# A symmetric block matrix built in pairs: the second sum of a pair goes into the tile of a loaded block

## The chip, the cores and the metric

The kernel runs on one NeuronCore of a Trainium2 chip. The metric is the device time of one execution in microseconds (us). The median of four runs before the change is 1603.98 us (1599.13 to 1610.67). The engines are named as in the profile: PE is TensorE (matmuls; PEld its weight loads), DVE is VectorE, ACT is ScalarE, POOL is GpSimd, SP is SyncE, which here only issues DMAs.

## What is computed

A graph convolution with a residual and a layer norm. Cut to what matters:

```python
HW = einsum('bnf,fo->bno', x, W)            # x: 8 x 4096 x 256, W: 256 x 256
A_norm = relu((A + A.T) * 0.5)              # A: 4096 x 4096, mostly zeros
D = sum(A_norm, axis=1)
d = where(D > 0, D ** -0.5, 0)
L_norm = eye(N) - d[:, None] * A_norm * d[None, :]
out = relu(einsum('nm,bmo->bno', L_norm, HW))
result = layernorm(x + out)
```

All numbers are float32 (f32).

## The kernel before

It has two large stages.

**Stage one** reads A in blocks of 512 by 512 (an 8 by 8 grid; one block is 1 MB and one tile of 128 partitions by 4 times 512 numbers) and writes relu((A + A.T)/2) into a scratch matrix in device memory, `a_dram`. The loop runs over the block row i and, inside it, over j from i to 7. For j > i the two blocks (i,j) and (j,i) are handled together and are called a pair here. One pair goes like this:

- `load_adj` loads the blocks, `tij` first and `tji` second, from SP's DMA queue (line 350), into the pool `adj` of four buffers. For j = i there is one load, and `tji` is `tij`.
- `symmetrise` forms one sum: for each of the four row strips of a block, PE transposes four 128 by 128 pieces of the opposite block into one bank of PSUM (line 360), and DVE adds the block's own strip to it (line 364), into the sum's tile. The transposes take banks from four of the tag `b0`, which other matmuls share, so PE can be at most four strips ahead of DVE.
- `keep` then takes the finished sum: ACT applies the relu with factor 0.5 in place (line 368), DVE reduces it to the sums of groups of 64 columns, `part` (line 369), ACT's DMA queue stores it to `a_dram` (line 375), and for j = i POOL copies the diagonal pieces to `diag`.

Each sum has a tile of its own in the pool `sym` of three buffers, so a pair takes two. The sum of block (i,j) comes first and that of (j,i) second; both are formed before `keep` is called for either, but with other work recorded between (below). A buffer is free again for a load or a sum when everything that reads or writes its old tile is done; a store counts until it has landed.

Beside each pair stand matmuls that don't depend on it. `form` makes 128 rows of x times W: two loads of x (line 451, SP's queue for i below 4, POOL's from i = 4 on), transposes on PE (`xtr`, line 458), copies by ACT (`xt`, line 459), matmuls (`pg`, line 469), and the eviction by ACT. Where the degree of these rows is known the eviction scales by r (`gt`, line 479) and the result is stored to `g_dram`; the last ten strips (22 to 31) are formed early, kept unscaled (`held`, line 481) and scaled once r is known (`release`, lines 492 and 494). `multiply` adds up the product for the first 128 rows of the output (`lead`, line 427), one strip at a time. For i below 4 there is about one `form` per pair, from i = 4 on two.

After row i, `degrees(i)` sums row i of `part` (line 386) and makes r with a power on POOL (line 389), and `lower_diagonal` subtracts from the diagonal pieces and stores them. In rows 3 and 4 `spread_early` makes index lists for stage two in tiles that it takes from the same two pools: `hot` from `sym`, `mixed` from `adj`.

The order on each engine is not written by hand in stage one: a scheduler sets it from the recorded order and its own estimate of times. On an engine and on its DMA queue, instructions are issued strictly in that order, so a load that waits for its buffer holds up what stands behind it. The DMAs of SP and ACT take one of eight completion semaphores in turn, and each waits until the DMA that had the semaphore before it has landed.

**Stage two** starts when `a_dram` and `g_dram` are complete. For each 128 rows of the output it gathers the nonzero rows by indirect DMAs from POOL (lines 733 and 744) and multiplies (`py`, line 933), and applies the residual and the layer norm.

Of the kernel before, what the change touches and what calls it, by code (L numbers as in the profile page):

```python
# [9 lines left out]
F32 = mybir.dt.float32  # L10
# [34 lines left out]
def kernel(  # L45
# [28 lines left out]
    P = 128  # L74
    S = 512
    A = S // P
# [100 lines left out]
    def patterns(u):  # L177

        used = ipool.tile([P, QU, NB], F32, tag="used", name=f"used_{u}", bufs=1)
        nb = blocks(u)  # L180
        if nb == 1:
            nc.vector.memset(used, 0.0)
        lo = (2 * u + 1) * 2
        nc.vector.tensor_scalar(
            used[:, : 2 * nb],
            part[:, :, lo : lo + 2 * nb].rearrange("p m s -> p s m"),
            0.0,
            None,
            ALU.is_gt,
        )  # L190
        diag = used[:, :, 2 * u + 1 : 2 * u + 1 + nb]
        nc.vector.tensor_tensor(diag, diag, own[:, :, :nb], ALU.max)
        two = ipool.tile([P, 2, NB], F32, tag="two", name=f"two_{u}", bufs=1)
        uv = used.rearrange("p (b h) m -> p b h m", b=2)
        nc.vector.scalar_tensor_tensor(two, uv[:, :, 1], 2.0, uv[:, :, 0], ALU.mult, ALU.add)
        pat = ipool.tile([P, NB], F32, tag="pat", name=f"pat_{u}")
        nc.vector.scalar_tensor_tensor(pat, two[:, 1], 4.0, two[:, 0], ALU.mult, ALU.add)
        kind = ipool.tile([P, NK, NB], BF16, tag="kind", name=f"kind_{u}")
        nc.vector.tensor_tensor(
            kind,  # L200
            pat.unsqueeze(1).to_broadcast([P, NK, NB]),
            kinds.unsqueeze(2).to_broadcast([P, NK, NB]),
            ALU.is_equal,
        )
        plan[u] = pat, kind
# [128 lines left out]
    with (  # L334
# [13 lines left out]
        def load_adj(i, j):  # L348
            t = apool.tile([P, A, S], F32, tag="adj", name=f"adj_{i}_{j}")
            nc.sync.dma_start(  # L350
                t,
                adj[i * S : (i + 1) * S, j * S : (j + 1) * S].rearrange("(a p) s -> p a s", p=P),
            )
            return t

        def symmetrise(i, j, tij, tji, sym):
            for a in range(A):
                pt = psum.tile([P, S], F32, tag="b0", name=f"tr_{i}_{j}_{a}")
                for c in range(A):
                    ins = nc.tensor.transpose(  # L360
                        pt[:, c * P : (c + 1) * P], tji[:, c, a * P : (a + 1) * P], ident
                    )
                done_pe.append(ins.ins)
                nc.vector.tensor_add(sym[:, a, :], pt, tij[:, a, :])  # L364
                yield

        def keep(i, j, sym, diag):
            nc.scalar.activation(sym, sym, AF.Relu, scale=0.5)  # L368
            nc.vector.tensor_reduce(  # L369
                part[:, i * A : (i + 1) * A, j * S // Q : (j + 1) * S // Q],  # L370
                sym.rearrange("p a (c q) -> p a c q", q=Q),
                AX.X,
                ALU.add,
            )
            nc.scalar.dma_start(
                a_dram[i * S : (i + 1) * S, j * S : (j + 1) * S].rearrange("(a p) s -> p a s", p=P), sym
            )
            if i == j:
                for a in range(A):
                    nc.gpsimd.tensor_copy(diag[:, a, :], sym[:, a, a * P : (a + 1) * P])  # L380

        def degrees(i):
            ms = slice(i * A, (i + 1) * A)
            deg = stat1.tile([P, A], F32, tag="deg", name=f"deg_{i}")
            none = stat1.tile([P, A], F32, tag="none", name=f"none_{i}")
            nc.vector.tensor_reduce(deg, part[:, ms, :], AX.X, ALU.add)
            nc.vector.tensor_scalar(none, deg, 0.0, None, ALU.is_le)
            nc.vector.tensor_add(e[:, ms], deg, none)  # L388
            nc.gpsimd.tensor_tensor(r[:, ms], e[:, ms], neg_half[:, :A], ALU.pow)  # L389
            nc.vector.tensor_scalar(minus_r[:, ms], r[:, ms], -1.0, None, ALU.mult)  # L390
# [34 lines left out]
        def multiply(m, g, strip):  # L425
            for c in range(G // S):
                nc.tensor.matmul(  # L427
                    lead[c],
                    lhsT=strip,
                    rhs=g[:, c * S : (c + 1) * S],  # L430
                    start=not done,
                    stop=len(done) == NB - 1,
                    skip_group_check=True,
                )
                yield
            done.append(m)
# [63 lines left out]
        def release_all(i):  # L500
            for m in range(i * A, (i + 1) * A):
                if m in held:
                    release(m)
            lower_diagonal(i, diags.pop(i))
# [8 lines left out]
        def run_due(flush=False):  # L513
            for d in due:
                d[0] -= 1
            while due and (flush or due[0][0] <= 0):
                _, fn, args = due.pop(0)
                fn(*args)
# [29 lines left out]
        for i in range(NS):  # L548
            diag = stat1.tile([P, A, P], F32, tag="diag", name=f"diag_{i}")
            for j in range(i, NS):  # L550
                tij = load_adj(i, j)
                tji = load_adj(j, i) if j > i else tij
                parts = [(i, j, tij, tji)] + ([(j, i, tji, tij)] if j > i else [])
                parts = [(p, spool.tile([P, A, S], F32, tag="sym", name=f"sym_{p[0]}_{p[1]}")) for p in parts]
                credit += (1.0 if j > i else 0.5) * (1 if i < 4 else 2)
                beside = [multiply(*args) for args in waiting]
                waiting.clear()
                products = len(beside)

                some = i < NS - 2 or i == j  # L560
                while some and credit >= 1.0 and (known or early):
                    beside.append(form(known.pop(0), True, i >= 4) if known else form(early.pop(0), False))
                    credit -= 1.0
                    some = i < NS - 2
                credit = min(credit, 1.0)
                for p, sym in parts:
                    for _ in symmetrise(*p, sym):
                        pass
                if i == NS - 1:


                    release_all(i - 1)
                    beside = beside[products:] + beside[:products]
                for n, b in enumerate(beside):
                    with tc.issue_after(done_pe[-1]) if i == NS - 1 and n < 2 else nullcontext():
                        for _ in b:
                            pass
                for (rows, cols, _, _), sym in parts:
                    keep(rows, cols, sym, diag)
                run_due()  # L580
            degrees(i)
            diags[i] = diag
            if i != NS - 2:
                release_all(i)
            known += range(i * A, min((i + 1) * A, NB - HOLD))
            if i == 1:
                for n, u in enumerate(SEQ[:2]):
                    patterns(u)
                    due += [[2 + n, count_place, (u,)], [4 + n, count_place_rest, (u,)]]
                due.sort(key=lambda d: d[0])  # L590
            elif i == 2:
                for n, u in enumerate(SEQ[2:4]):
                    patterns(u)
                    due.append([1 + n, count_place, (u,)])
                due.append([3, count_place_rest, (SEQ[2],)])
            elif i < 5 and i > 2:

                pieces = spread_early(SEQ[i - 3])
                for n in range(5):
                    due.append([1 + n // 2, next, (pieces, None)])  # L600
                due.append([4, collect_index, (SEQ[i - 3],)])
# [10 lines left out]
    def residual(i, ypool):  # L612
        xr = ypool.tile([P, B, F], F32, tag="xr", name=f"xr_{i}", bufs=4)
        ins = nc.scalar.dma_start(xr, x[:, i * P : (i + 1) * P, :].rearrange("b p f -> p b f"))
        return xr, ins.ins
# [343 lines left out]
    with tc.If(short > 0):  # L959
        with (  # L960
# [4 lines left out]
            for i in range(NB):  # L965
# [17 lines left out]
                z, _ = residual(i, ypool)  # L983
# [30 lines left out]
```

## Time and profile before

The profiled execution took 1604.0 us; its span, from the first to the last instruction of the core, is 1602.3 us.

| engine | busy us | share of the span | instructions |
|---|---|---|---|
| PE matmul | 1498.1 | 93% | 6544 |
| PE weight loads | 779.8 | 49% | 6544 |
| DVE | 890.9 | 56% | 2250 |
| ACT | 371.6 | 23% | 462 |
| POOL | 759.8 | 47% | 1109 |

| stage | window, us | PE busy us | DVE busy us | DMA share | GB/s |
|---|---|---|---|---|---|
| one | 0 to 575 | 527.65 | 362.47 | 0.97 | 359 |
| two | 575 to 1603 | 970.49 | 528.46 | 0.95 | 359 |

The mean granted clock of TensorE is 0.972. The DMA share is the mean busy share of the core's 16 DMA engines, from the time that their packets took; it can come out a little above 1.

What the steps of stage one cost each:

| line | step | count | mean ns |
|---|---|---|---|
| L360 | PE transpose, 128x128 | 1024 | 285 |
| L364 | DVE addition, 128x512 | 256 | 683 |
| L368 | ACT relu, 128x2048 | 64 | 1914 |
| L369 | DVE reduction, 128x2048 to 128x32 | 64 | 2278 |
| L469 | PE matmul, 128x256 | 1024 | 383 |
| L427 | PE matmul `lead`, 128x512 | 176 | 593 |

Each of the 64 loads of A and each of the 64 stores to `a_dram` moves 1024 KB.

### The profile page before, as it was taken

To read this page: it belongs to the slowest core of one execution; us is meant where nothing else is said; L and a number is where in the kernel's file an instruction comes from. 1 tells how busy PE (TensorE), PEld (TensorE's weight loads), DVE (VectorE), ACT (ScalarE), POOL (GpSimd) and SP (SyncE) were. 2 spreads that over 40 slices of the span, in tenths; PEclk is the share of its full clock that TensorE was granted. 3 is DMA by queue.
4 is the path that set the end of the run, shared out by engine and by line. 5 is a ranking of instruction groups with operands and counts; after the bars stand their busy time and mean duration, and the time that the engine had idled before them with its cause. 6 is when DMAs were issued, how large, how long until landed. Compare 5 with 4: busy or idle time off the path is not lost.

```text
span 1602.3 us, 18959 instructions
## 1 busy us (share of the span) xinstructions
PE 1498.1 (93%) x6544; PEld 779.8 (49%) x6544; DVE 890.9 (56%) x2250; ACT 371.6 (23%) x462; POOL 759.8 (47%) x1109
## 2 busy tenths in 40 slices
PE   6999989998899898999999998899999998999984
PEld 5778877777677633333333333234333342333331
DVE  5665668876474604355384493571085655657542
ACT  3555554554344500101001000010001101010111
POOL 3001010102123256576776676676576666666662
PEclk9999999999999998999999999899999998999997
DMA  9999999999889899999999999999899999999994
GB/s 355 367 362 404 389 363 377 398 391 367 291 325 330 343 356 403 355 389 347 404 368 367 377 372 357 374 386 362 322 347 346 345 377 361 377 384 374 361 342 157
DMA packets 222037, 575.71 MB, mean 359 GB/s; under 512 B 20403, under 2 KB 108771, under 8 KB 184195
## 3 DMA queue, kind: packets, MB, share of 16 engines
q0 software_dynamic: 59552, 316.19, 51.3%
q10 hardware_dynamic: 72032, 134.51, 22.2%
q1 hardware_dynamic: 90352, 123.74, 22.0%
q8 instruction: 54, 0.88, 0.2%
q14 instruction: 47, 0.39, 0.1%
HBM read 479.07 MB, written 136.34 MB: 384 GB/s over the span
## 4 chain that ended last, share of the span: by engine, by line
PE 74%; DMA 12%; DVE 8%; issue 3%; ACT 2%; POOL 0%; SPq 0%; ACTq 0%; DVEq 0%; POOLq 0%
PE py L933 53%; PE pg L469 10%; DMA a_dram<-sym 5%; PE lead L427 5%; DMA g<-g_dram,gi 3%; DVE sym L364 3%; PE xtr L458 3%; PE tr L360 3%; DMA adj<-in_adj_dram 2%; DVE part L369 1%; DMA xin<-in_x_dram 1%; ACT sym L368 1%; DMA xr<-in_x_dram 1%; PE lists L295 1%; ACT xt L459 0%
## 5 line engine op out<-in xcount | busy, mean ns | idle before, releaser
L933 PE MATMUL py<-g,ga 128*64 128x512 f32 (+1 forms) x3152 | 946.1, 603 | 38.9 <-issue 24.4
L933 PEld LDWEIGHTS py<-g,ga 128*64 128x64 f32 (+1 forms) x3152 | 343.2, 154 | 630.2 <-issue 602.1
L744 POOL DMA_INDIRECT g<-g_dram,gi x302 | 339.1, 1123 | 238.3 <-issue 76.4
L733 POOL DMA_INDIRECT ga<-a_dram,ai x302 | 331.5, 1098 | 99.7 <-issue 86.5
L631 DVE TENSOR_TENSOR xr<-xr,y 128x2048 f32<-128x2048 f32 x31 | 71.1, 2294 | 452.9 <-ACT y L620 378.7
L620 ACT ACTIVATE y<-py,minus_r 128x512 f32<-128x512 f32 x120 | 80.5, 687 | 889.2 <-PE py L933 837.4
L469 PE MATMUL pg<-w_sb,xt 128*128 128x256 f32 x1024 | 230.8, 383 | 5.3 <-ACT xt L459 5.2
L364 DVE TENSOR_TENSOR sym<-tr,adj 128x512 f32<-128x512 f32 x256 | 163.3, 683 | 112.5 <-PE tr L360 93.0
L469 PEld LDWEIGHTS pg<-w_sb,xt 128*128 128x128 f32 x1024 | 194.4, 193 | 33.7 <-ACT xt L459 6.0
L369 DVE TENSOR_REDUCE part<-sym 128x32 f32<-128x2048 f32 x64 | 145.4, 2278 | 62.4 <-ACT sym L368 62.4
L360 PE MATMUL tr<-ident,adj 128*128 128x128 f32 x1024 | 137.6, 285 | 24.4 <-DVE sym L364 12.0
L389 POOL TENSOR_TENSOR r<-e,neg_half 128x4 f32<-128x4 f32 x8 | 8.3, 1040 | 317.4 <-DVE e L388 304.6
L368 ACT ACTIVATE sym<-sym 128x2048 f32<-128x2048 f32 x64 | 122.5, 1914 | 121.4 <-DVE sym L364 121.4
L360 PEld LDWEIGHTS tr<-ident,adj 128*128 128x128 f32 x1024 | 119.8, 146 | 52.4 <-DVE sym L364 23.9
L636 DVE BATCH_NORM_STATS2 stats<-xr 128x6 f32<-128x256 f32 x256 | 87.3, 412 | 19.4 <-POOL xr L631 18.3
L458 PE MATMUL xtr<-ident,xin 128*128 128x128 f32 x512 | 72.1, 287 | 16.6 <-DVE sym L364 15.9
L660 DVE TENSOR_SCALAR xr<-xr,mv,root 128x256 f32<-128x256 f32 x248 | 83.8, 410 | 0.1
L427 PE MATMUL lead<-gt,strip 128*128 128x512 f32 x176 | 82.5, 593 | 0.0
L459 ACT COPY xt<-xtr 128x512 f32<-128x512 f32 x128 | 69.3, 590 | 40.4 <-PE xtr L458 38.6
L479 ACT ACTIVATE gt<-pg,r 128x512 f32<-128x512 f32 x88 | 60.5, 688 | 76.9 <-PE pg L469 72.6
L458 PEld LDWEIGHTS xtr<-ident,xin 128*128 128x128 f32 x512 | 59.4, 146 | 33.2 <-DVE sym L364 26.1
L274 DVE TENSOR_TENSOR hot<-iota_q,at 128x1024 bf16<-128x1024 f32 x64 | 74.2, 1219 | 2.1 <-DMA a_dram<-sym 2.1
(114 smaller groups left out, 579.3 us busy)
## 6 DMA issues: line engine op xcount, KB each, us to landing
adj<-in_adj_dram SPq DMA_DIRECT2D x64, 1024.0 KB
a_dram<-sym ACTq DMA_DIRECT2D x64, 1024.0 KB
xr<-in_x_dram ACTq DMA_DIRECT2D x32, 1024.0 KB
out_dram<-xr SPq DMA_DIRECT2D x31, 1024.0 KB
xin<-in_x_dram SPq DMA_DIRECT2D x44, 512.0 KB
g_dram<-gt ACTq DMA_DIRECT2D x22, 1024.0 KB
xin<-in_x_dram POOLq DMA_DIRECT2D x20, 512.0 KB
g_dram<-held ACTq DMA_DIRECT2D x10, 1024.0 KB
```

The lines of the kernel that those rows point to most:

```text
L360: ins = nc.tensor.transpose(pt[:, c * P : (c + 1) * P], tji[:, c, a * P : (a + 1) * P], ident)
L364: nc.vector.tensor_add(sym[:, a, :], pt, tij[:, a, :])
L368: nc.scalar.activation(sym, sym, AF.Relu, scale=0.5)
L369: nc.vector.tensor_reduce(part[:, i * A : (i + 1) * A, j * S // Q : (j + 1) * S // Q], sym.rearrange("p a (c q) -> p a c q", q=Q), AX.X, A ...
L427: nc.tensor.matmul(lead[c], lhsT=strip, rhs=g[:, c * S : (c + 1) * S], start=not done, stop=len(done) == NB - 1, skip_group_check=True,)
L458: nc.tensor.transpose(pt[:, k, c, :], xin[b // H][:, b % H + k, c * P : (c + 1) * P], ident)
L469: ins = nc.tensor.matmul(pg[:, k * FO : (k + 1) * FO], lhsT=xt[:, b + k, c, :], rhs=w_sb[:, c, :], start=(c == 0), stop=(c == FC - 1),)
L636: nc.vector.bn_stats(stats[:, b, :], z[:, b, :])
L660: nc.vector.tensor_scalar(z[:, b, :], z[:, b, :], mv[:, b, 0:1], rstd[:, b : b + 1], ALU.subtract, ALU.mult,)
L733: nc.gpsimd.indirect_dma_start(out=at if both else at[:, :P], out_offset=None, in_=a_pairs if both else a_rows, in_offset=bass.IndirectOff ...
L744: nc.gpsimd.indirect_dma_start(out=gt, out_offset=None, in_=g_dram, in_offset=bass.IndirectOffsetOnAxis(ap=gi[:, t : t + 1], axis=0), boun ...
L933: last_product = nc.tensor.matmul(py[2 * u + 1 + b][c][rows, :], lhsT=at[:, off + rows.start : off + rows.stop], rhs=gt[:, c * S : (c + 1) ...
```

## The change

```diff
@@ -550,8 +550,9 @@
             for j in range(i, NS):
                 tij = load_adj(i, j)
                 tji = load_adj(j, i) if j > i else tij
-                parts = [(i, j, tij, tji)] + ([(j, i, tji, tij)] if j > i else [])
-                parts = [(p, spool.tile([P, A, S], F32, tag="sym", name=f"sym_{p[0]}_{p[1]}")) for p in parts]
+
+                sym = spool.tile([P, A, S], F32, tag="sym", name=f"sym_{j}_{i}")
+                parts = [((j, i, tji, tij), sym)] + ([((i, j, tij, tji), tij)] if j > i else [])
                 credit += (1.0 if j > i else 0.5) * (1 if i < 4 else 2)
                 beside = [multiply(*args) for args in waiting]
                 waiting.clear()
```

A pair now takes one tile of the pool `sym` instead of two. The two sums change places: the sum of block (j,i), which is `tji` plus the transposed `tij`, comes first and goes into the `sym` tile. The sum of block (i,j), which is `tij` plus the transposed `tji`, comes second and is written over `tij` itself. By then the transposes that read `tij` have been issued for the first sum. The relu, the reduction and the store of the second sum then work on that tile of the pool `adj`. For j = i there is still one sum, in a `sym` tile. The pools keep their numbers of buffers, four and three; what is added, reduced and stored is the same.

## The prediction

> **What bounds the kernel now.** I read the windows first, then the waits of SP's queue and of VectorE up to 575 us, then the timeline around the few places where TensorE stands still.
>
> ```profile
> 13.00:120.00 107.00, 97.62 (x577) 83.27 (x578) 70.83 (x82) 57.49 (x71) 6.40 (x68) 0.97 1.03 368
> 129.00:222.00 93.00, 91.51 (x531) 74.91 (x530) 59.00 (x72) 50.56 (x61) 4.82 (x10) 1.00 1.04 391
> 368.00:446.00 78.00, 66.77 (x370) 53.66 (x369) 42.67 (x54) 33.04 (x40) 13.23 (x21) 0.93 0.81 299
> 575.00:1603.00 1028.00, 970.49 (x3672) 362.92 (x3670) 528.46 (x1721) 90.37 (x136) 674.90 (x609) 0.97 0.95 359
> ```
>
> Columns: window, length, busy time of TensorE (PE), its weight loads, VectorE (DVE), ScalarE (ACT), GpSimd (POOL), granted clock, DMA share, GB/s. The change touches only the stage that forms the symmetric matrix, 0 to about 575 us. Within it TensorE is busy 97.6 of 107 and 91.5 of 93 us, with the DMA share above 1 beside it: two full resources, so little is to be had. Only around 368 to 446 us is there slack on both.
>
> ```profile
> SPq L350 <- DVE sym L364: 343.7, 42, 25.1
> ...
> DVE sym L364 <- PE tr L360: 93.0, 20, 16.4
> DVE part L369 <- ACT sym L368: 62.4, 18, 6.2
> DVE sym L364 <- DMA a_dram<-sym: 12.4, 7, 6.9
> ...
> PE xtr L458 <- DVE sym L364: 15.9, 17, 4.6
> ```
>
> Who <- whom: total us, times, longest. The fourth row is what the change can remove: seven times a sum waits until the store of an older sum has left one of the three sum buffers, 12.4 us in all. The first row says that the loads of A already stand waiting for buffers, so their lead is what the change spends.
>
> **What it removes.** With one sum tile per pair instead of two, three buffers cover three pairs, so all 12.4 us of that wait go from VectorE. What of it reaches TensorE:
>
> ```profile
> 366.53 3.19 DVE L364 TENSOR_TENSOR sym<-tr,adj 128x512 f32<-128x512 f32 x5 [2.37 <-DMA a_dram<-sym]
> ...
> 375.08 2.82 PE L458 MATMUL xtr<-ident,xin 128*128 128x128 f32 x12 [4.64 <-DVE sym L364]
> ...
> 438.48 0.69 DVE L364 TENSOR_TENSOR sym<-tr,adj 128x512 f32<-128x512 f32 x1 [6.92 <-DMA a_dram<-sym]
> ```
>
> Pair (3,7): VectorE starts 2.37 us earlier, and the 4.64 us hole of TensorE behind it is VectorE's queue, so 2.4 us come off; bounds 0 and 2.4. Pair (4,7): 6.92 us go, but the next load, block (5,5), is late in their place. Before, it was issued at 429.8 us, once (4,6) had been added, and landed at 440.1 (landing: the sixteenth update of the load's semaphore in the trace). Now its buffer is the one that (4,7)'s first sum and second transposes release, about 5.5 us after that pair begins at 434.2, so 439.7. Loads issued near there took 5.9 us (428.1 to 434.0), 6.6 and 10.3; it lands at 445.6 to 450, where TensorE took it up at 445.9. So its start stays or slips by up to 4 us; in return the reductions of (4,7), which spread the four sums of (5,5) over 448.3 to 454.6 us (four take 2.5), are over by then: up to 3.8 us back. Bounds -3.8 and +4; I take -2, since the two nearest loads took 6 us. The other five waits share 12.4 - 6.9 - 2.4 = 3.1 us, in a stretch with DMA share 1.03; bounds 0 and 3.1, taken -1.5.
>
> A rule of the Trainium skill speaks against this last term. DMA: Bandwidth & Descriptors, Specifications, gives some 358 GB/s from HBM per core. By it row 0 of A, at 368 GB/s, is already at its limit and the term is 0. The trace has 391 GB/s over 93 us, so I do not hold to it.
>
> **What it costs elsewhere.** The sums themselves cost the same: 683 ns for the 128x512 addition, 1914 ns for the relu, 2278 ns for the reduction, 64 stores as before, only the destination differs. So the price is in waits and in order.
>
> First, the loads. In the changed program the four loaded-block buffers are handed on so: the second block of pair k frees its buffer after the pair's first sum and second transposes, about 5.5 us into the pair, and that goes to the first block of pair k+2; the first block now frees its buffer only when the store of the second sum has landed, and that goes to the second block of pair k+2. Behind that load on SP's queue stand the next first block and two loads of x. Take pair (1,3): it begins at 144.7 us, its second store issues at 157.9 and lands at 166.2. The second block of (1,5), issued at 150.3 before, is issued at 166.2. Loads that found SP's queue nearly empty took 6.7 (166.0 to 172.7), 7.2 and 5.2 us, so it lands at about 173.5; pair (1,5) begins at 176.7 and adds it 0.6 us later. Likewise: store of (1,4) lands at 183.4, needed at 193.0; (1,5) at 199.2, needed at 206.0; (2,4) at 265.9, needed 276.2; (2,5) at 282.1, needed 291.9; (3,4) at 335.8, needed 345.6; (3,5) at 352.8, needed 361.6. The leads left are 6.8 to 11 us against 5.2 to 7.2 for the load. So I book 0, hidden behind the pair between; if loads took the 10 to 12 us that those queued second took before (182.9 to 192.4, 198.4 to 208.5), each of the 15 pairs of rows 1 to 3 would be up to 2 us late: bounds 0 and +30. In row 0 the planner pairs the buffers differently: the second block of (0,k+1) follows the first sum of (0,k), 5.5 us into a pair of 14.4, lead 9.5 us. That holds too, but for (0,3), whose second block waits for the store of (0,1), landed at 38.9: with 7 us it lands at 45.9, 0 to 1.5 us late, taken +0.5.
>
> A late block would cost more than its delay where it stops TensorE:
>
> ```profile
> 226.80:229.60 2.80, 0.07 (x2) 0.03 (x1) 2.80 (x4) 0.00 (x0) 0.16 (x1) 0.99 1.04 405
> 229.60:233.00 3.40, 3.40 (x16) 3.40 (x17) 3.40 (x6) 2.48 (x2) 0.00 (x0) 0.50 0.87 302
> ```
>
> TensorE stood 2.7 us, and the next 3.4 us were granted half the clock, some 1.7 us of work lost. The skill's TensorE: Matmul & The Clock Gate, Why this matters for your kernels, puts the danger at gaps above some 3 us. By that rule a block 2 us late costs 2; by this row one 2.7 us late costs 4.4, so the rule's limit is too kind here.
>
> Second, the order of the two sums is swapped: block (j,i) is first, and (i,j), which belongs to row i, second. The row's degree needs all of row i, so it now follows the last pair's second reduction. For rows 0 to 4 the scale r is not read until several us later (r of row 0 was ready at 114.7, first read at 124.6; shifted by some 7 us it is still in time), booked 0. For row 5 TensorE had waited 1.04 us for the scaled tiles; the changed order puts other matmuls ahead, 0 to -1, booked 0. Row 6 is tight:
>
> ```profile
> 538.07 2.27 DVE L369 TENSOR_REDUCE part<-sym 128x32 f32<-128x2048 f32 x1
> ...
> 538.71 2.00 ACT L494 ACTIVATE held<-held,r 128x2048 f32<-128x2048 f32 x1 [1.37 <-POOL r L389]
> ...
> 542.51 2.00 ACT L494 ACTIVATE held<-held,r 128x2048 f32<-128x2048 f32 x1 [1.80 <-DVE held L492]
> ...
> 545.55 7.83 PE L469 MATMUL pg<-w_sb,xt 128*128 128x256 f32 x24 [5.19 <-ACT xt L459]
> ```
>
> Now: four sums of (7,7) from 535.2 to 537.7, the second reduction to 540.0, three small instructions to 540.8, r on GpSimd (1.04) to 541.8, two scalings on ScalarE (2.0 each, without the 1.8 us hole) to 545.9, then the copies of xt: TensorE resumes at about 546.7 instead of 545.55. +1.2, and every gather behind it moves with it; bounds 0 and +3.
>
> **Sum.** -2.4 - 2 - 1.5 + 0.5 + 1.2 = -4.2 us. The profiled execution's span is 1602.3 us and its time 1604.0, so 1598.1 and 1599.8; its time is the median of the runs shown (1603.98). The stage of gathers from 575 us on is unchanged in its order and only shifts. Forecast: 1600 us.
>
> **Rivals.** Bound for "no change": 0.5%, 8 us, about what repeated runs of this kernel (1599.1 to 1610.7) can tell; so below 1596 is faster, above 1612 slower.
>
> Slower: the store-to-load chain sets the pace in rows 1 to 3. A second sum is stored (8 to 11 us), its buffer loaded (7 to 12), transposed and added (5), and stored again some 9 to 14 us later in ScalarE's order. It turns once in two pairs, 32 us. With store and load at 9 and 9 it closes in 32; from 18 us for the two together it decides. At 11 and 10 it needs 35 to 36, 1.5 to 2 us per pair, 15 pairs, 22 to 30 us, less what is gained: about 1620, or 1612 if half the pairs slip. For it: DMA share 1.04, and stores of 10.8 and 11.5 us at 134 and 138 us. Against it: fewer loads in flight make each shorter.
>
> Faster: the removed waits pay in full and take half-clock windows with them. At 372.9 and 441.2 us the clock was halved for 6.8 us each behind the two holes (0.50 in those windows), 3.4 us of work each. 12.4 + 3.4, less 1.2, gives -14.6: 1589; with only (3,7) and (4,7) in full and one half window, -2.4 - 6.9 - 3.4 + 1.2 = -11.5: 1592. Against it: the load of (5,5).
>
> That the change does nothing: the waits are only the other side of a full DMA, and the first sum then waits for its loaded blocks instead: -6 to +4 about 1604. It falls in the same class as the forecast.
>
> **How the numbers follow.** Forecast and "does nothing" together 0.43 (own range 1596 to 1611), slower 0.30, faster 0.27. The time is that of the likeliest, 1600. The range 1588 to 1621 reaches into both others and leaves some 0.07 below and 0.11 above.
>
> **What would show it.** Right: no row of sums waiting for the store; SP's wait under the loads ended by stores or reductions; TensorE waits for loaded blocks a few us in all; the hole near 370 us below 3 us; (5,5) begun within 2 us of 446; stage two shifted as a whole. Wrong: repeated waits of TensorE's transposes or VectorE's sums for loads in rows 1 to 3, pairs further apart than 16 us, more half-clock windows.

## The result and the profile after

The changed kernel takes 1608.56 us (median of 43 runs, 1602.53 to 1619.11), the kernel before 1603.61 us (median of 69 runs beside them, 1596.0 to 1612.96). The ratio is 1.0035, 95% interval 1.0025 to 1.0046: 5.6 us slower (0.0035 times 1603.61), with 4.0 to 7.4 as the interval. The forecast was 1600, slightly faster; the time lies inside the range, but the likeliest case was wrong and the sign too. The profiled execution of the changed kernel took 1608.3 us with a span of 1606.6, 4.3 us more than before.

The same windows of the changed kernel, the last one to its later end, columns as above:

```profile
13.00:120.00 107.00, 100.13 (x586) 82.82 (x587) 71.36 (x84) 58.91 (x76) 4.74 (x69) 0.98 1.01 370
129.00:222.00 93.00, 88.86 (x495) 71.89 (x496) 55.11 (x66) 48.67 (x60) 3.27 (x7) 0.98 1.01 367
368.00:446.00 78.00, 69.05 (x381) 54.35 (x379) 45.84 (x62) 35.60 (x41) 13.71 (x21) 0.96 0.89 326
575.00:1606.00 1031.00, 975.41 (x3686) 361.81 (x3684) 528.71 (x1721) 90.60 (x136) 675.44 (x611) 0.98 0.95 358
```

Row 0 of A (first line) went better: TensorE is busy 2.5 us more in the same 107. Row 1 (second line) went worse: 88.9 of 93 us instead of 91.5, and 367 GB/s instead of 391. The waits up to 575 us (who <- whom, total, times, longest):

```profile
SPq L350 <- DMA a_dram<-adj: 260.3, 25, 32.2
SPq L350 <- DVE sym L364: 89.4, 19, 12.4
...
PE lead L427 <- DMA strip<-a_dram: 2.9, 1, 2.9
...
PE xtr L458 <- DMA xin<-in_x_dram: 1.3, 1, 1.3
```

No sum waits for a store any more: the row of 12.4 us is gone. The loads now stand 260 us behind stores, as was to be expected, and at a loaded block of A TensorE hardly waits more than before (12.1 us against 11.3). What is new is small and stands elsewhere: 2.9 us once for a strip, and 1.3 us once for rows of x (0.4 before).

To see where the time went I took, from both traces, the first transpose of every pair and compared them. In us, changed kernel minus kernel before, one profiled execution each:

| from ... to | ahead or behind at its end | lost (+) or won (-) in it | booked |
|---|---|---|---|
| start to (1,2), row 0 | -4.0 | -4.0 | -1.0 (part of the other waits -1.5, and +0.5) |
| (1,2) to (1,3) | +0.8 | +4.8 | 0 |
| (1,3) to (3,7) | +3.1 | +2.2 | 0 (bounds 0 to +30) |
| (3,7) to (4,5) | +3.2 | +0.1 | -2.4 |
| (4,5) to (5,6) | +0.9 | -2.3 | -2 |
| (5,6) to (6,7) | +3.6 | +2.7 | 0 |
| (6,7) to the first product of stage two | +5.8 | +2.2 | +1.2 |

The end of the span is 4.3 us later, so stage two only shifted, by a microsecond or two less. Most of the loss lies in three places: behind row 0, row 5 and row 6. Behind row 0, timeline of the kernel before and then of the changed one (start, duration, engine, line, what, [idle before <- what ended it]):

```profile
115.45 2.41 POOL L401 DMA_DIRECT2D a_dram<-diag  x4 [0.77 <-DVE diag L398]
...
121.25 4.32 POOL L417 DMA_DIRECT2D strip<-a_dram  x8 [3.39 <-DMA a_dram<-diag]
...
132.62 3.60 PE L427 MATMUL lead<-gt,strip 128*128 128x512 f32 x8
```

```profile
119.40 2.41 POOL L401 DMA_DIRECT2D a_dram<-diag  x4 [0.97 <-DVE diag L398]
...
125.52 0.55 POOL L417 DMA_DIRECT2D strip<-a_dram  x1 [2.96 <-DMA a_dram<-diag]
...
131.65 5.40 PE L427 MATMUL lead<-gt,strip 128*128 128x512 f32 x8 [2.86 <-DMA strip<-a_dram]
```

The degree of row 0 is ready later, so the diagonal pieces are stored 3.95 us later, and the `strip` that holds one of them, a 128 by 128 piece of `a_dram` that `lead` multiplies by, is loaded 4.3 us later. Before, its load landed at 127.1 us (sixteenth update of its semaphore) and was first read at 132.6: 5.6 us in hand. Now it lands at 131.6, and TensorE, 4 us ahead thanks to row 0, wants it at 128.8. It stands 2.86 us, and the eight matmuls behind the hole take 5.40 instead of 3.60 us: 4.7 of the 4.8 us. Behind row 5 of the kernel before, and then behind rows 5 and 6 of the changed one:

```profile
510.82 7.13 PE L427 MATMUL lead<-held,strip 128*128 128x512 f32 x16 [1.04 <-ACT held L494]
...
519.53 7.07 PE L469 MATMUL pg<-w_sb,xt 128*128 128x256 f32 x32
```

```profile
510.62 2.28 DVE L369 TENSOR_REDUCE part<-adj 128x32 f32<-128x2048 f32 x1
...
513.54 1.09 PE L458 MATMUL xtr<-ident,xin 128*128 128x128 f32 x8 [1.99 <-DVE sym L364]
514.47 4.54 PE L469 MATMUL pg<-w_sb,xt 128*128 128x256 f32 x12
...
541.59 2.27 DVE L369 TENSOR_REDUCE part<-adj 128x32 f32<-128x2048 f32 x1
...
545.88 2.00 ACT L494 ACTIVATE held<-held,r 128x2048 f32<-128x2048 f32 x1 [4.67 <-POOL r L389]
...
551.54 7.63 PE L469 MATMUL pg<-w_sb,xt 128*128 128x256 f32 x24 [7.43 <-ACT xt L459]
```

Row 5: the late reduction of (5,7) now stands between the second and third of the four additions of (6,6), which hold the PSUM banks that `xtr` needs. Before, 16 `lead` matmuls on `held` covered that time; their scaled tiles are now late too. TensorE waits 1.99 us instead of 1.04, and the next 12 `pg` matmuls take 4.54 us where 12 of the usual 32 in 7.07 us take 2.65. Row 6: the hole before `pg` is 7.43 us instead of 5.19.

### The profile page after: what moved, and what is told of

Same layout as the page of the kernel before. It is cut to its first block, busy times and chain, and to the rows that moved or that the text cites. A ratio compares the mean times of both kernels' runs of the same rounds, so it can differ in the third digit from the quotient of the medians.

```text
span 1606.6 us, 18940 instructions
## 1 busy us (share of the span) xinstructions
PE 1501.8 (93%) x6544; PEld 776.3 (48%) x6544; DVE 890.5 (55%) x2250; ACT 369.6 (23%) x462; POOL 758.4 (47%) x1109
## 4 chain that ended last, share of the span: by engine, by line
PE 74%; DMA 9%; issue 8%; DVE 4%; another core or an unknown queue 2%; ACT 1%; POOL 1%; SPq 0%; POOLq 0%; ACTq 0%; DVEq 0%
PE py L934 53%; PE pg L469 9%; PE lead L427 5%; PE tr L360 3%; DMA g<-g_dram,gi 3%; PE xtr L458 3%; DMA adj<-in_adj_dram 2%; DVE sym L364 1%; DMA a_dram<-adj 1%; DVE part L369 1%; DMA xr<-in_x_dram 1%; DMA xin<-in_x_dram 1%; PE lists L295 1%; ACT adj L368 0%
## 5 line engine op out<-in xcount | busy, mean ns | idle before, releaser
L934 PEld LDWEIGHTS py<-g,ga 128*64 128x64 f32 (+1 forms) x3152 | 339.5, 154 | 632.4 <-issue 593.9
L745 POOL DMA_INDIRECT g<-g_dram,gi x302 | 333.0, 1103 | 239.4 <-issue 78.1
L734 POOL DMA_INDIRECT ga<-a_dram,ai x302 | 335.7, 1112 | 99.4 <-issue 85.9
L360 PE MATMUL tr<-ident,adj 128*128 128x128 f32 x1024 | 136.2, 283 | 25.3 <-DMA adj<-in_adj_dram 12.1
L364 DVE TENSOR_TENSOR sym<-tr,adj 128x512 f32<-128x512 f32 x144 | 93.2, 683 | 111.5 <-PE tr L360 92.0
L369 DVE TENSOR_REDUCE part<-adj 128x32 f32<-128x2048 f32 x28 | 63.9, 2282 | 55.6 <-ACT adj L368 55.6
L368 ACT ACTIVATE sym<-sym 128x2048 f32<-128x2048 f32 x36 | 68.9, 1915 | 108.2 <-DVE sym L364 105.2
L417 POOL DMA_DIRECT2D xin<-in_x_dram x20 | 15.5, 776 | 164.9 <-PE xtr L458 164.2
L369 DVE TENSOR_REDUCE part<-sym 128x32 f32<-128x2048 f32 x36 | 82.0, 2278 | 10.0 <-ACT sym L368 10.0
```

Source lines behind the costliest of these rows:

```text
L360: ins = nc.tensor.transpose(pt[:, c * P : (c + 1) * P], tji[:, c, a * P : (a + 1) * P], ident)
L369: nc.vector.tensor_reduce(part[:, i * A : (i + 1) * A, j * S // Q : (j + 1) * S // Q], sym.rearrange("p a (c q) -> p a c q", q=Q), AX.X, A ...
L734: nc.gpsimd.indirect_dma_start(out=at if both else at[:, :P], out_offset=None, in_=a_pairs if both else a_rows, in_offset=bass.IndirectOff ...
L745: nc.gpsimd.indirect_dma_start(out=gt, out_offset=None, in_=g_dram, in_offset=bass.IndirectOffsetOnAxis(ap=gi[:, t : t + 1], axis=0), boun ...
L934: last_product = nc.tensor.matmul(py[2 * u + 1 + b][c][rows, :], lhsT=at[:, off + rows.start : off + rows.stop], rhs=gt[:, c * S : (c + 1) ...
```

## The experiments

All of these kernels compute the whole result. Kernels of one group ran on one chip, beside the kernel before; that took 1606.11 us on the chip of the first group and 1596.78, 1597.13 and 1596.72 on those of the other three. So differences are taken from the ratio on the same chip, never between groups in absolute time. The theories: **A**, the swapped order of the two sums makes what hangs on a row's degree late; **B**, loads wait for the store of the second sum; later **C**, the order of loads on SP's queue, and **D**, a DMA that is full whoever issues.

**Group 1: which half of the change.** Order alone (`e1_order_only`; both sums in tiles of their own):

```diff
-                parts = [(i, j, tij, tji)] + ([(j, i, tji, tij)] if j > i else [])
+                parts = ([(j, i, tji, tij)] if j > i else []) + [(i, j, tij, tji)]
```

> The kernel before with only the order of a pair's two sums swapped, both still in sum tiles of their own. Theory A (the swap of the order costs: each row's degree, diagonal blocks and scaled tiles come one sum later): row 0 keeps its pace here, so the first strip, which lay ready 5.6 us before it was read, comes some 4 us later and still in time; rows 5 and 6 lose 2.5 us each as in the changed kernel, so before + 4 to + 7: 1608 to 1611 us. Theory B (a loaded block waits for the store of the second sum, which now lies in a loaded block's buffer): nothing here waits for that, so before within 2: 1602 to 1606 us.

Measured: ratio 1.0081 (1.0053 to 1.0108), +13.0 us. Theory B predicted nothing and falls as the sole cause; A has the direction but is too small. The pace shows why: behind row 5 it loses 8.7 us, not 2.5. Timeline of this kernel:

```profile
513.67 0.69 DVE L364 TENSOR_TENSOR sym<-tr,adj 128x512 f32<-128x512 f32 x1 [6.95 <-DMA a_dram<-sym]
...
514.42 1.11 PE L458 MATMUL xtr<-ident,xin 128*128 128x128 f32 x4 [4.67 <-DVE sym L364]
```

Without the in-place sum the first sum of (6,6) waits 6.95 us for a store. So the in-place half of the change is a gain here, and hides part of what the order costs. In row 0 the strip came 1.5 us late, not in time.

The in-place half alone, in the old order (`e2_inplace_old_order`):

```diff
-                sym = spool.tile([P, A, S], F32, tag="sym", name=f"sym_{j}_{i}")
-                parts = [((j, i, tji, tij), sym)] + ([((i, j, tij, tji), tij)] if j > i else [])
+                sym = spool.tile([P, A, S], F32, tag="sym", name=f"sym_{i}_{j}")
+                parts = [((i, j, tij, tji), sym)] + ([((j, i, tji, tij), tji)] if j > i else [])
```

> Second sum in place, but in the order of before: (i,j) first in a sum tile, (j,i) second into the tile of block (j,i). Theory A: the gain in row 0 (4.2 us) stays and nothing is late behind the rows, so before - 4 to - 7: 1597 to 1600 us, with no wait of the lead product for its first strip and a hole near 545 us of about 5 us. Theory B: a load waits for a store here as well, so as the changed kernel, 1607 to 1611 us.

Measured: ratio 1.0008 (0.9984 to 1.0031), +1.3 us, with -2.6 to +5.0 as the interval. That excludes the time of A (-4 to -7), not that of B (1607 to 1611 us, which is +3 to +7 on the kernel before). A's local signs are there (no wait for the strip, the hole before `pg` 5.20 us, 3.7 us ahead at (1,3)), but the lead is lost again, 1.3 and 4.5 us on the way to (1,6) and (1,7):

```profile
190.45 3.98 PE L360 MATMUL tr<-ident,adj 128*128 128x128 f32 x32 [1.12 <-DMA adj<-in_adj_dram]
...
198.58 1.94 PE L458 MATMUL xtr<-ident,xin 128*128 128x128 f32 x8 [3.07 <-DMA xin<-in_x_dram]
```

Block (6,1) is loaded into the buffer of (4,1)'s sum, whose store landed at 181.7; it was issued at 182.1 and landed at 190.3, 1.1 us late. Two loads of x, issued behind it and another block from 183.1 on, landed 3 us late. This is B, in one place, and the queue behind it.

The changed kernel with the old order only in the last pair of each row (`e3_last_pairs_old`):

```diff
-                sym = spool.tile([P, A, S], F32, tag="sym", name=f"sym_{j}_{i}")
-                parts = [((j, i, tji, tij), sym)] + ([((i, j, tij, tji), tij)] if j > i else [])
+                one, two = ((i, j, tij, tji), (j, i, tji, tij)) if j == NS - 1 else ((j, i, tji, tij), (i, j, tij, tji))
+                sym = spool.tile([P, A, S], F32, tag="sym", name=f"sym_{one[0]}_{one[1]}")
+                parts = [(one, sym)] + ([(two, two[2])] if j > i else [])
```

> The changed kernel with the old order in the last pair of each row alone. Theory A: only these pairs feed the degree, so all that is late behind the rows comes back: 1597 to 1601 us. Theory B: 26 of the 28 second sums... of the 28 pairs 21 are as in the changed kernel and in all 28 a load waits for a store, so 1607 to 1610 us.

Measured: ratio 0.9979 (0.9956 to 1.0002), -3.4 us; the expectation of A is at its upper edge, that of B is excluded. Seven pairs in another order undo the loss. (With the order, the block whose tile takes the second sum changes too in these pairs: (7,i) instead of (i,7).) Timeline of this kernel behind row 0 and row 6:

```profile
128.38 3.60 PE L427 MATMUL lead<-gt,strip 128*128 128x512 f32 x8
...
543.08 8.42 PE L469 MATMUL pg<-w_sb,xt 128*128 128x256 f32 x24 [5.19 <-ACT xt L459]
```

TensorE now reads the strip at 128.4 without a wait, and the hole is 5.19 us again. It still loses 2.1 us at (1,7).

The same for the pair (0,7) alone (`e4_row0_last_old`; the condition above is `i == 0 and j == NS - 1`):

> The changed kernel with the old order in the pair (0,7) alone. Theory A: the lead product's wait for its first strip (2.9 us) and the half clock behind it (1.8 us) go, the rest stays: 4 to 5 us below the changed kernel, 1603 to 1605 us, and pair (1,3) begins near 141 us instead of 145.5. Theory B: the wait for the strip is one of a crowded DMA and stays: 1607 to 1610 us.

Measured: ratio 1.0027 (1.0006 to 1.0049), +4.3 us, only some 1.3 below the changed kernel, which the intervals cannot tell from nothing. The time is the one that B gave, but its reason is not: the wait for the strip is gone. Pair (1,3) begins at 140.8, as A said, 4.7 us earlier than in the changed kernel; but 1.8 us go at (1,5), in a wait of 1.59 us for x, and 1.6 at (2,4). The lead is won as foreseen and not kept.

**Group 2: more lead for the loads.** With the second sum in place, a pair needs one sum buffer. These versions have five buffers for loaded blocks and two for sums:

```diff
-        tc.tile_pool(name="adj", bufs=4) as apool,
-        tc.tile_pool(name="sym", bufs=3) as spool,
+        tc.tile_pool(name="adj", bufs=5) as apool,
+        tc.tile_pool(name="sym", bufs=2) as spool,
...
-            hot = spool.tile([P, A, S], F32, tag="sym", name=f"hot_{u}")
+            hot = apool.tile([P, A, S], F32, tag="adj", name=f"hot_{u}")
```

On the changed kernel (`e5_changed_5_2`):

> The changed kernel with the eighth KB-block of memory moved: five buffers for loaded blocks, two for sums, and the tile of the early spread that lay in a sum buffer put into a loaded block's buffer. Theory A (order): what is late behind rows 0, 5 and 6 stays, so no more than 2 to 3 us below the changed kernel (its slips of rows 1 to 3): before + 1 to + 4. Theory B (load behind store): a load has a pair more of lead, so all of the loss goes, before - 4 to - 8.

Measured: ratio 1.0018 (1.0008 to 1.0028), +2.9 us. That is A: the slip at (1,7) falls from 1.1 to 0.1, what is late behind the rows stays (strip 3.08 us, hole 7.42).

On the version with the old order in the last pairs (`e6_last_old_5_2`):

> The same split of the buffers (five and two) on the version with the old order in the last pair of each row. Theories A and B together (the order cost what e3 gave back, and the 2.1 us lost at pair (1,7) and 1.2 at (2,4) there are loads behind stores): before - 5 to - 8, pair (2,4) 4 us ahead of the kernel before. If the DMA itself is the limit in rows 1 to 3, the lead gained in row 0 is lost again whatever the buffers are: as e3, before - 1 to - 4.

Measured: ratio 0.9981 (0.9971 to 0.9991), -3.0 us, faster than before but no better than with four and three buffers, and 2.0 us are still lost at (1,7), now in a wait of 2.2 us for x. So the lead of the blocks was not what was short there, and A and B together asked for too much.

The kernel before, as a control (`e7_before_5_2`):

> The kernel before with the same split of the buffers (five and two). If the split alone helps: before - 2 to - 5. If two sum buffers cover only one pair there, so that every sum waits for the store of the pair before: VectorE waits for stores in most of the 28 pairs, 2 to 5 us each, before + 30 to + 100.

Measured: ratio 1.0363 (1.0344 to 1.0381), +58 us; VectorE waits 24 times for stores, 48.3 us in all. With two tiles per pair the split does not pay; the in-place sum is what frees the buffer.

The version with the old order in all pairs (`e8_old_order_5_2`):

> The same split on the version with the old order in all pairs. Theory B: the 5.8 us lost at pairs (1,6) and (1,7) (a wait of 1.1 us for block (6,1), then 3.1 us for the rows of x queued behind it) go: before - 4 to - 7. If the DMA itself is the limit there: before - 2 to + 3, as e2.

Measured: ratio 0.998 (0.9969 to 0.999), -3.2 us. The wait for block (6,1) is gone, as B said, but a wait for x remains:

```profile
196.61 1.06 PE L458 MATMUL xtr<-ident,xin 128*128 128x128 f32 x8 [2.07 <-DMA xin<-in_x_dram]
```

**Group 3: who waits on SP's queue.** In row 1 the loads of x for the three strips that are formed early, six loads of 512 KB, were put on GpSimd's queue; the others stay on SP's (`e9_last_old_5_2_x_row1`):

```diff
-                    beside.append(form(known.pop(0), True, i >= 4) if known else form(early.pop(0), False))
+                    beside.append(form(known.pop(0), True, i >= 4) if known else form(early.pop(0), False, i == 1))
```

> The version with the old order in the last pairs and five and two buffers, its loads of x in row 1 issued from GpSimd's queue instead of SP's. Theory C (order of the queue: in row 1 two loads of x stand on SP's queue behind a load of A that waits for the store of a second sum, landed at 179.0, and TensorE then waits 2.2 us for them at 193): the 2.0 us lost at pair (1,7) go, so 1.5 to 3 us below that version, before - 4.5 to - 7. Theory D (the DMA is full in row 1, whoever issues): the wait moves to a block of A, nothing gained, before - 2 to - 4.

Measured: ratio 0.9938 (0.9921 to 0.9954), -9.9 us. C, and more than it asked for: nothing is lost at (1,7). But its profiled executions reach stage two only 1.5 us (here) and 3.4 us (f4, below) earlier than that of the version with x on SP's queue (e6), so half or more of the 7 us between the two is not explained by this place.

The same for all loads of x from row 1 on (`e10_last_old_5_2_x_rows`; `i >= 1` in both calls):

> The same with the loads of x of rows 1 to 3 from GpSimd's queue. Theory C: at least as good as the version with row 1 alone, and the smaller slips at (2,4) and (3,6) (0.7 us each) go as well: before - 5 to - 8. Theory D: before - 2 to - 4; if GpSimd's queue, which also issues the strips, is late by it, TensorE waits for strips and the time is above before.

Measured: ratio 0.9937 (0.992 to 0.9953), -10.1 us: no better than row 1 alone. The lead of 5.8 us at (2,2) drops by 3.3 at (2,4).

With four and three buffers (`e11_last_old_x_row1`):

> The version with the old order in the last pairs, four and three buffers as in the changed kernel, and the loads of x of row 1 from GpSimd's queue. Theory C: of the 2.1 us lost at (1,7), which there are a wait of 1.5 us for block (7,1), part goes, as this block's load no longer shares the queue with x: before - 3 to - 6. Theory B alone (the block waits for the store): the wait for block (7,1) stays, before - 2 to - 4.

Measured: ratio 0.9968 (0.9953 to 0.9983), -5.1 us. The time is C's; but in the profiled execution the wait for block (7,1) is there and longer (4.18 us), as B said. Inconclusive between the two.

In place in row 0 alone, all else as before (`e12_row0_inplace`):

```diff
-                parts = [(p, spool.tile([P, A, S], F32, tag="sym", name=f"sym_{p[0]}_{p[1]}")) for p in parts]
+                parts = [(p, p[2] if i == 0 and p[0] > p[1] else spool.tile([P, A, S], F32, tag="sym", name=f"sym_{p[0]}_{p[1]}")) for p in parts]
```

> The kernel before with the second sum in place, old order, in row 0 alone; from row 1 on every sum has a sum tile as before. Theory B: the 4 us gained in row 0 are kept, since from (1,3) on no load waits for a second sum's store, pair (2,4) some 4 us ahead: before - 3 to - 5. Theory D (DMA full): TensorE meets late blocks in row 1 anyway and the lead is gone by (2,4): before - 1 to + 2.

Measured: ratio 1.0029 (1.0017 to 1.0041), +4.6 us, worse than both expectations. Ahead by 4.2 us at (1,3), it loses 7.8 at one place:

```profile
155.28 1.94 PE L458 MATMUL xtr<-ident,xin 128*128 128x128 f32 x8 [6.56 <-DMA xin<-in_x_dram]
```

That load of x was issued from 134.1 to 137.6 us and landed at 155.1, behind loads of A that were issued at 123.7, 128.6 and 130.8 us and landed at 138.7, 143.9 and 150.1. So loads of A that came out earlier stood in front of x. B has a part in it all the same: the load issued at 123.7 had waited for the store of an in-place sum of row 0, which landed at 123.6. SP's queue in this kernel from 117 to 125 us:

```profile
SPq L350 <- DMA a_dram<-adj: 5.5, 1, 5.5
```

How the loss divides between that store and the crowd of loads is not shown.

**Group 4: what was still open.** Does the queue limit the kernel before too, and what does the order alone cost where the loads are in time? The kernel before with the early loads of x of row 1 from GpSimd's queue (`f1_before_x_row1`):

> The kernel before, nothing in place, with the loads of x in row 1 from GpSimd's queue alone. Theory C' (SP's queue in row 1 limits the kernel before too): before - 3 to - 6, without any in-place sum. Theory E (the queue matters only once the lead gained in row 0 has to be kept): TensorE lost nothing in row 1 of the kernel before (pairs 15.6 to 16.4 us apart), so before - 1 to + 1.

Measured: ratio 1.0004 (0.9989 to 1.0018), +0.6 us: theory E; C' is excluded. Moving x gains nothing by itself.

The changed kernel with it (`f2_changed_x_row1`):

> The changed kernel with the loads of x in row 1 from GpSimd's queue. Theory A: what is late behind rows 0, 5 and 6 (4.8, 2.7 and 2.2 us) stays, only the slip at (1,7) goes: before + 2 to + 5. Theory C' : before - 3 to + 1.

Measured: ratio 1.0008 (0.9995 to 1.002), +1.3 us, with an interval that touches both. In its profiled execution the strip (2.96 us) and the hole (7.42) stay. The wait for x at (1,7) goes, and in its place block (7,1), of the same pair, is late (it landed at 208.9):

```profile
208.94 2.48 DVE L364 TENSOR_TENSOR sym<-tr,adj 128x512 f32<-128x512 f32 x4 [3.11 <-DMA adj<-in_adj_dram]
...
209.69 3.31 PE L360 MATMUL tr<-ident,adj 128*128 128x128 f32 x16 [3.41 <-DVE sym L364]
```

The changed kernel with five and two buffers and x of row 1 from GpSimd's queue, and the best version again, which differs from it by the order in the last pairs alone (`f3_changed_5_2_x_row1`, `f4_best_again`):

> The changed kernel with five and two buffers and the loads of x in row 1 from GpSimd's queue: the best version but for the order of the sums. Theory A: 7 to 10 us above the best version on the same chip (the lateness behind rows 0, 3, 5 and 6), so before - 2 to + 2. If the order cost only where the loads were late too: within 4 of the best version.

> The best version (old order in the last pairs, five and two buffers, x of row 1 from GpSimd's queue) on the same chip as the three others, for comparison: before - 7 to - 12 by its earlier runs; by its stage one alone (3.5 us ahead at the first product of the gathers) before - 3 to - 6.

Measured: 0.9995 (0.9984 to 1.0005), -0.8 us, and 0.9937 (0.992 to 0.9953), -10.1 us. The order in seven pairs costs the difference, 9.3 us, as A said. The changed order behind row 0, and then the best version at pair (1,7):

```profile
132.87 5.40 PE L427 MATMUL lead<-gt,strip 128*128 128x512 f32 x8 [2.81 <-DMA strip<-a_dram]
```

```profile
191.28 2.46 PE L458 MATMUL xtr<-ident,xin 128*128 128x128 f32 x16
```

In the first the strip is late again. In the best version row 1 runs without a wait at the place where the old-order version of group 2 waited 2.07 us for x. Its two profiled executions (e9 and f4) reach stage two 3.5 and 5.4 us ahead of the kernel before's; where the other 5 to 7 us of its gain lie is not settled, since the kernel before was not profiled on that chip.

## Why the prediction was wrong

**Bound, removed waits in row 0.** "Little is to be had" was wrong for row 0, where TensorE stood 9.4 of the 107 us: -4.0 us came where about -1 was booked. The 14 profiled executions with the in-place sum in that row are 2.8 to 5.5 us ahead at (1,1), 4.0 in the mean, in either order; e1 and f1, with sums in tiles of their own and the same buffers, are 2.1 and 0.9 ahead. So some 2 to 3 us belong to the sum itself, as an estimate: these are single executions, and one and the same kernel was 2.8 us ahead in e9 and 5.5 in f4. In the changed kernel one microsecond is a half-clock window at 35 us that did not come; four waits for stores, 2.4 us in all, went.

**Pair (3,7), booked -2.4.** Wrong, +0.1. VectorE's wait of 2.37 us went, and the hole behind shrank only from 4.64 to 4.02 us:

```profile
371.79 0.69 DVE L364 TENSOR_TENSOR sym<-tr,adj 128x512 f32<-128x512 f32 x1 [1.84 <-PE tr L360]
372.40 2.28 DVE L369 TENSOR_REDUCE part<-sym 128x32 f32<-128x2048 f32 x1
374.59 2.28 DVE L369 TENSOR_REDUCE part<-adj 128x32 f32<-128x2048 f32 x1
...
377.52 0.66 PE L458 MATMUL xtr<-ident,xin 128*128 128x128 f32 x4 [4.02 <-DVE sym L364]
```

VectorE was done earlier and then waited 1.84 us for the transposes of (4,4); the two reductions still stand in its order before the other sums that free the banks. The wait moved, the queue did not.

**Pairs (4,7) and (5,5), booked -2.** Right in size: -2.3 from (4,5) to (5,6). With the order put back it is -1.0 (e3), with the order alone -0.1 (e1), so it seems to have taken both halves; one execution each does not show more. The load of (5,5) was issued at 442.6, not at 439.7, and landed at 448.3, TensorE took it at 448.46, inside the bounds 445.6 to 450, and the pair began 2.5 us after 446, where the list of signs allowed 2.

**Loads behind stores, booked 0.** In the changed kernel itself nearly right: of the 2.2 us lost in rows 1 to 3, some 1.1 are at (1,7), from a wait of 1.3 us for x, the queue behind the block that the prediction named. But the zero held, as it seems, only because TensorE had just lost its lead at the strip: where it kept the lead (e2, old order in place), the same chain cost 5.8 us. (The two queued loads to which the prediction gives 10 to 12 us took 9.5 and 10.2.) The slower rival's place was therefore right, its weight in this kernel not: the store-to-load chain did not set the pace (most pairs of rows 1 to 3 are 15.6 to 16.8 us apart, as before).

**The order of the sums: the step that failed.** "For rows 0 to 4 the scale r is not read until several us later (...) booked 0": I followed r to the eviction that reads it, in row 0 alone, and left out the other thing that hangs on the degree, the diagonal pieces, their store, and the strip that is loaded back for `lead`. That chain had 5.6 us in hand; being late by 4.5 and the gain of row 0 used it up: +4.8. Row 0 had 9.9 us in hand for r, but row 2 had only 1.8 (ready at 303.6, read at 305.4). There the eviction now waits for r, and the transposes of (3,4) wait for the eviction; the kernel before first, then the changed one:

```profile
305.36 0.69 ACT L479 ACTIVATE gt<-pg,r 128x512 f32<-128x512 f32 x1 [1.14 <-issue]
```

```profile
309.51 0.69 ACT L479 ACTIVATE gt<-pg,r 128x512 f32<-128x512 f32 x1 [3.58 <-POOL r L389]
...
313.21 0.66 PE L360 MATMUL tr<-ident,adj 128*128 128x128 f32 x4 [0.27 <-ACT gt L479]
```

Pairs (3,4) and (3,5) slip by 0.8 and 0.4 us, and this wait of 3.6 us is there, in all six versions with the swapped order at the end of row 2 and in none with the old one. Row 5, "0 to -1, booked 0", was +2.7: the held scaling was indeed moved behind other matmuls, but the reduction that comes late went in among the additions of (6,6). Row 6, +1.2, was the right mechanism and mis-sized: +2.2, inside its bounds. Together that is 4.8 + 2.7 + 2.2 + 1.2 = 10.9 us, of which 1.2 was booked; the runs f3 and f4 put the order at 9.3. The places agree: f3 loses 4.8 behind row 0, 1.2 in row 3, 1.9 behind row 5 and 2.9 behind row 6, while f4 loses nothing at any of them. Nothing else in the sum is off by as much.

**Signs.** Of those named, the vanished wait for stores, SP's waits ended by stores, few waits for blocks and the shifted second stage came; the hole near 370 us below 3 us did not. None of them looked at the strip or the turn of a row, where the loss was.

**Rivals.** Faster: a gain of 10 us, near its time, came only with the order and x put right; how much of it the removed waits pay is not shown. "Does nothing" came nearest in time, but by luck: the waits did pay in row 0, and the order took it back.

**Open.** The slip of about 1 us at (2,4), which comes in both orders; where the rest of the best version's gain lies; and f1's profiled execution, 9.9 us behind at the start of stage two while its median is level. It was the slowest of f1's twelve runs (1603.19 us, median 1598.62), and 5.1 of the 9.9 us come at (2,2), where an addition waits 3.28 us for a store that took 13 us to land: one execution of a kernel is not its median.

## What to carry to other kernels

An in-place result changes which input must come last, and so the order of the results: before anything else, list all that hangs on each result (here scales, diagonal, a strip read back), with the time in hand for each, at the pace that the change itself brings, not at the old one. Keep the old order where a result closes a row, and swap it elsewhere if the buffers ask for it. And a lead that is won at one place must be fed on: look at what stands in the load queue behind the load that will now be asked for earlier.

## What the runs showed of the hardware

TensorE was granted half its clock behind holes well under 3 us: behind 2.86 us (eight `lead` matmuls 5.40 instead of 3.60) and behind 1.99 us (window from 515.0 us in the changed kernel). No sharp limit shows. At one and the same place, near 32 us, a hole of 1.74 us had half clock behind it in the kernel before and none in e1, and one of 1.68 in the changed kernel had none; nor had one of 2.27 us at 450.7 us in the kernel before (granted clock 1.00 from 449 to 458). The Trainium skill (TensorE: Matmul & The Clock Gate, Why this matters for your kernels) puts the danger above some 3 us; these rows put it lower, at least for some holes.

The kernel before took 9 us less on the chips of groups 2 to 4 than on that of group 1. In the profiles of those groups the first 788 products of stage two take 12.5 us less than in the kernel before's, whatever was changed in stage one.
